# Where two chunks' layer-3 projections are asked for: in the first attention block of layer 1, or ahead of its group norm

## The chip, the cores and the metric

One core of a Trainium2 chip runs the whole program. Its engines work side by side, each through a queue of its own in order: PE (TensorE, matrix products), DVE (VectorE), ACT (ScalarE), POOL (GpSimd), and SP (SyncE), which here issues DMAs. The metric is the device time of one execution in microseconds (us); lower is better. Everything is float32.

## What is computed

Four layers on four images of 64 x 64 pixels with 128 channels. Layer 0 is neighbourhood attention with a 7 x 7 window, layer 1 a group norm and full attention over all 4096 pixels, layer 2 a gated mixing with a layer norm, layer 3 a scan in four directions (behind a projection and a 3 x 3 depthwise convolution). Cut to what this change touches:

```python
x = L0(x)                                  # neighbourhood attention
# layer 1
h = group_norm(x, gn_scale, gn_bias)       # 32 groups, statistics over a whole image
q, k, v = h @ wq + bq, h @ wk + bk, h @ wv + bv
o = softmax(q k^T / sqrt(128)) v
x = x + o @ wo + bo
x = L2(x)
# layer 3, its front
xz = x @ Win                               # 128 -> 512
xb, z = split(xz)                          # 256 channels each
xb = silu(depthwise_conv_3x3(xb) + conv_b)
...                                        # four scans, gate by silu(z), layer norm, Wout
```

The group norm needs the mean and the variance over a whole image, so layer 1 of an image can't begin before the last block of its layer 0.

## The kernel before

The images go one after the other through layers 0 to 2, and the scan of layer 3 comes behind all of them. What layer 3 needs before its scan (projection, convolution, gate, in the program "the front") is spread over the attention of layer 1: while image `b` is in layer 1, the front works on the second half of the image ahead (`b - 1`, chunks 4 to 7) and on the first half of `b`. A chunk is 8 image rows, 512 pixels. For image 0 there is no image ahead, so the first four places of the front are empty there.

Layer 0 of an image (`layer_0`) takes 32 blocks of 128 pixels. For each it makes scores (PE, L458), adds the bias and takes the maximum (DVE, L462), the exponential (ACT, L476), divides (POOL, L484), transposes the weights (PE, L493; copied out by ACT or DVE at L495), multiplies with the values (PE, L504; ACT L509) and projects (PE, L514; DVE L515). Every fourth block four finished tiles are transposed into `hT` (PE L413, ACT L414) and their statistics taken (DVE L417). Many of these instructions are pinned to the order in which the program asks for them.

Layer 1 (`layer_1`) then does the group norm, a chain of small steps that wait for each other: L556 (DVE, statistics of the image) -> L559 (PE, over groups) -> L561, L563, L565 (DVE) -> L567 (PE) -> L569 (DVE) -> L570 (ACT, square root, with a load of its table ahead of it) -> L572, L573 (DVE) -> L582 (DVE, eight times, the normalised `hT`) -> L584, L587, L591 (PE, queries, keys and values of eight chunks). After that come 32 blocks of attention: `score` (PE L613, copied out by ACT L616, maximum on DVE L619, L624), `turn_maxima` (PE L628, DVE L630 and L632), `soften` (PE L636, DVE L639, ACT L640) and `value` (PE L646). The maximum of a block is turned during the block behind it, and its values are multiplied in the block behind that one, so block 0 has scores alone and block 1 scores and the turn.

Behind block `i` the function `between(i)` asks for work of layer 2 and calls `first_part(i)`, which is the front's `turn(i)`. In a turn, `project` makes a chunk's projection: two matmuls (L788, 128x512, two records in the trace each), two copies into the tile `xh` (ACT L789) and the rows at the seam to the neighbouring chunk (POOL L792 to L795). `convolve` asks for the convolution of a chunk in four parts: ACT begins the sum (L831) and makes four of the nine products (L846, L850), POOL adds those (L858, L861), and DVE does the other four (L867, `add_taps`, called "taps" below). `gate` (L817) is the other half of the projection. `add_parts` asks for the POOL additions of the turn before.

The order within an engine's queue is not that of the program text: a scheduler places an instruction where it expects its inputs, by the order of the asking, except for those that are pinned. What is asked for early can so be placed early, with all that hangs on it.

The tiles of the front lie in the places of layer 0's bias tables (`xh` in the place "be", the sums `acc` in "bm0" and "bm2"), so nothing can be written into `xh` before layer 0's last L462 has read its bias.

Before the change, `first_part(-1)` loads the two chunks (L782) ahead of `layer_1`, and `turn(0)`, behind block 0, projects them:

```python
        first_part = front(b)
        first_part(-1)
        layer_1(b, xt, *handed.pop(b), between)
```

Of the kernel before, what the change touches and what calls it, by code (L numbers as in the profile page):

```python
# [75 lines left out]
def region(n, dy, dx):  # L76

    return max(0, -dy - RC * n), min(RC, H - dy - RC * n), max(0, -dx), min(W, W - dx)
# [60 lines left out]
def layers_0_to_2(  # L139
# [619 lines left out]
    def by_image_rows(t):  # L759
        return t.rearrange("p (i j) -> p i j", j=W)  # L760

    def front(b):
# [6 lines left out]
        def at_end(i, n):  # L769
            return i == B - 1 and n >= 4  # L770

        def by_product(i, n):


            return n == 3 or at_end(i, n)

        def load(i, n):
            if at_end(i, n):
                x_of[i, n] = fresh.pop(n)
                return  # L780
            x = x_of[i, n] = tmp.tile([P, CH], F32, name="xc", tag="g1")
            nc.sync.dma_start(x, x3_d[i][:, bass.ts(n, CH)])  # L782

        def project(i, n):
            me = n & 1
            for f in range(2):
                pi = ps_s([P, CH], "pi")
                nc.tensor.matmul(pi, lhsT=win[:, P * f:P * f + P], rhs=x_of[i, n], start=True, stop=True)  # L788
                nc.scalar.copy(xh[:, me, f, 1:RC + 1, :], by_image_rows(pi))  # L789
            row = nc.vector if at_end(i, n) and n > 5 else nc.gpsimd  # L790
            if n == 4 and i < b:
                nc.gpsimd.tensor_copy(xh[:, me, :, 0, :], kept_row)  # L792
            elif n > 0:
                row.tensor_copy(xh[:, me, :, 0, :], xh[:, 1 - me, :, RC, :])
                row.tensor_copy(xh[:, 1 - me, :, RC + 1, :], xh[:, me, :, 1, :])  # L795

        def project_row(i, n):

            me = n & 1
            x = tmp.tile([P, W], F32, name="xr", tag="oT")  # L800
            nc.sync.dma_start(x, x3_d[i][:, CH * n:CH * n + W])
            pi = ps_t([P, 2, W], "pr3")
            for f in range(2):
                nc.tensor.matmul(pi[:, f, :], lhsT=win[:, P * f:P * f + P], rhs=x, start=True, stop=True)
            nc.scalar.copy(xh[:, 1 - me, :, RC + 1, :], pi)
            nc.gpsimd.tensor_copy(kept_row, xh[:, 1 - me, :, RC, :])
# [6 lines left out]
        def gate(i, n):  # L813
            x = x_of.pop((i, n))
            for f in range(2):
                pz = ps_s([P, CH], "pz")
                nc.tensor.matmul(pz, lhsT=win[:, DI + P * f:DI + P * f + P], rhs=x, start=True, stop=True)  # L817
                zf = tmp.tile([P, CH], F32, name="zf", tag="c512", bufs=9)

                silu(i, n, zf, pz)  # L820
                nc.sync.dma_start(zf_d[i][f][:, bass.ts(n, CH)], zf)
# [11 lines left out]
        def taps(i, n):  # L833


            v = (1, 0) if n < NCH - 1 else (-1, 0)
            gp, ve = [v, (-1, 1), (1, -1), (1, 1)], [(-v[0], 0), (0, -1), (0, 1), (-1, -1)]
            return (gp[:2], ve + gp[2:]) if i == B - 1 and n in (5, 7) else (gp, ve)
# [14 lines left out]
        def add_parts():  # L853
            for i, n, f, k, p in parts_of:
                of = taps(i, n)[0]
                r0, r1, c0, c1 = region(n, *of[k])
                a = by_image_rows(sums[n, f])[:, r0:r1, c0:c1]
                nc.gpsimd.tensor_tensor(a, a, p, ALU.add)  # L858
                if k == len(of) - 1:
                    acc = accs[n & 1][:, f, :]  # L860
                    nc.gpsimd.tensor_tensor(acc, acc, sums.pop((n, f)), ALU.add)  # L861
            parts_of.clear()
# [33 lines left out]
        def activate(i, n, apart=False):  # L896
            if apart:
                u_of[i, n] = [tmp.tile([P, CH], F32, name="u1", tag="c512", bufs=9) for _ in range(2)]
                for f in range(2):
                    if i == B - 1 and (n, f) in ((6, 0), (6, 1), (7, 0)):  # L900
                        nc.scalar.activation(u_of[i, n][f], sums.pop((n, f)), AF.Silu, bias=cl("conv_b", f))
                    else:
                        silu(i, n, u_of[i, n][f], accs[n & 1][:, f, :])
            else:
                u_of[i, n] = [u0[:, f, :] for f in range(2)]
                silu(i, n, u0, accs[n & 1])
# [6 lines left out]
        def copy_du(i, n):  # L913

            m = (L - CH * (n + 2)) // SC
            for f in range(2):
                for b2 in range(B):
                    if b2 != i - 1:
                        nc.sync.dma_start(y_d[(i ^ b2) >> 1][b2][f][m], y_d[(i ^ (i - 1)) >> 1][i - 1][f][m])
# [37 lines left out]
        def times_b(i, n, bb, engine):  # L957
            for f, u in enumerate(u_of.pop((i, n))):
                engine.tensor_tensor(u, u, bb, ALU.mult)
                nc.sync.dma_start(ub_d[i][f][:, bass.ts(n, CH)], u)  # L960
# [37 lines left out]
        takes = [[(b - 1, 4), (b - 1, 5)], [(b - 1, 6)], [(b - 1, 7)]] if b > 0 else [[], [], []]  # L998
# [4 lines left out]
        def convolve(i, n, fs, half):  # L1003
            for f in fs:
                if half == 0:
                    begin(n, f)
                multiply(i, n, f, range(len(taps(i, n)[0]))[2 * half:2 * half + 2])
            for f in fs if half else []:
                add_taps(i, n, f)
# [49 lines left out]
        def turn(i):  # L1059

            j, r = divmod(i, 4)
            add_parts()
            if i == -1:
                for c in takes[0]:
                    load(*c)
                return
            now = whole[j] if j < 8 else None
            if j < 8:
                if r == 0:
                    for c in takes[j]:  # L1070
                        project(*c)
                    if j == 7 and b < B - 1:
                        project_row(b, 4)
                if now and j < 7:
                    convolve(*now, (r // 2,), r & 1)
                elif now and r < 2:
                    convolve(*now, range(2), r)
                if r == 3:
                    for c in takes[j]:
                        gate(*c)  # L1080
                    for c in takes[j + 1] if j < 7 else []:
                        load(*c)

            for k, at in ((0, 16), (2, 28), (4, 32)):
                if i == at and whole[k] and whole[k][0] & 1:
                    copy_du(*whole[k])
            if b > 0 and i == 8 and (b - 1) & 1:
                copy_du(b - 1, 2)

            for c, at in zip(whole, u_at):  # L1090
                if c and i == at:
                    activate(*c, at >= 32)
                if c and i == at + 1:
                    lower(*c)
                if c and i == at + 2 and not by_product(*c):
                    times_b(*c, x_of.pop((*c, "b")), nc.gpsimd)
            if b > 0 and i in (22, 24):
                turn_c(b - 1, (i - 22) // 2)
            if b == 0 and i == 3:
                output_weights()  # L1100
            if b == B - 1 and i == 6:
                diagonals()
            if b == B - 1:
                end(i)
# [7 lines left out]
    for b in range(B):  # L1112
        xt = ahead.pop(0)
        for _ in coming:
            pass
        parts = layer_2(b, xt)

        def between(i):

            n, part = divmod(i - 6, 4)  # L1120
            if i == 6 and b + 1 < B:
                ahead.append(load_x(b + 1))
            if i >= 6 and n < NCH:
                parts[part](n)
            first_part(i)
            if b + 1 < B and i == NT + 1:
                edge_of[b + 1] = edge_bias(0)
            if b + 1 < B and i == NT + 3:
                bias_m[:] = bias_tiles()
                for t, d in zip(bias_m, bias_d):  # L1130
                    nc.sync.dma_start(t, d)

        first_part = front(b)
        first_part(-1)
        layer_1(b, xt, *handed.pop(b), between)
        if b + 1 < B:
            coming = layer_0(b + 1, ahead[0], edge_of[b + 1])
        for i in range(NT + 2, NT + 6 if b + 1 < B else NT + 11):
            between(i)
            if b + 1 < B:  # L1140
                next(coming)
                next(coming)
# [380 lines left out]
```

## Time and profile before

| | |
|---|---|
| median of 3 runs | 3720.32 us (3720.11 to 3721.49) |
| the profiled execution's own time | 3719.04 us |
| span of its instructions | 3717.3 us |
| busy in the span: PE, DVE, ACT, POOL | 90%, 75%, 73%, 38% |
| granted PE clock over the span | 0.916 |
| start of the group norm (L556), images 0 to 3 | 209.26, 933.95, 1684.75, 2435.65 us |
| first L582, images 0 to 3 | 212.31, 937.11, 1687.92, 2438.81 us |
| L788 | 592 ns a record, x112 (chunks read from DRAM) |

The page tells busy time by engine, then the span in 40 slices, queues, the chain that ended last, the costliest groups of instructions by line, and DMA issues. A line of the timeline reads: start in us, length in us, engine, line, operation, output<-input, shapes, how many, and in brackets the idle time ahead of it and what ended it. Lengths of neighbours overlap: the next of a row begins some 0.1 us before the end of the one ahead, so what a queue pays for one instruction is read from start to start. A table by stretches gives for each A:B (us from the span's start) its length, then for each engine the busy time and the number of instructions that began in it, the granted PE clock and the DMA share.

### The profile page before, as it was taken

Reading aid. Unit: us, or ns where it says so; the run is one execution under the profiler, and the core shown is the slowest. Engines: PE = TensorE matmul, PEld = TensorE weight load, DVE = VectorE, ACT = ScalarE, POOL = GpSimd, SP = SyncE. Lnnn points to the kernel's source line nnn. Section 1 sums busy time; section 2 is a strip of 40 time slices with the busy share of each in tenths; the row PEclk is TensorE's granted clock in tenths of the full one; section 3 lists DMA queues with packets and bytes.
Section 4 is the critical chain, followed back from the end, with each engine's and each line's share of the span. In section 5 each row is a group of like instructions: output and inputs, shape, how many; then the busy total and the mean of one; then the engine's idle time right before and its main releaser. Section 6 shows DMA issues by size and latency. Waiting matters only on the chain. (4 is left out here: it accounts for less than half of the span.)

```text
span 3717.3 us, 70142 instructions
## 1 busy us (share of the span) xinstructions
PE 3357.8 (90%) x26774; PEld 2775.6 (75%) x26774; DVE 2794.8 (75%) x5227; ACT 2700.4 (73%) x4387; POOL 1422.9 (38%) x1592
## 2 busy tenths in 40 slices
PE   6999999999999999998999999989999997666647
PEld 3779999967799999677999997779899962222236
DVE  3667878866677788666777886667787777999968
ACT  3865677778677777786677776867767778999934
POOL 5600012245121222451122223522221337999956
PEclk7999999999999999999999999999999995555579
DMA  4200000131011012410121212100100259999998
GB/s 130 63 3 26 13 18 30 45 99 40 10 49 35 32 41 82 127 45 1 47 77 30 72 51 98 47 1 24 43 31 33 70 168 240 219 232 210 210 275 281
DMA packets 188308, 310.95 MB, mean 84 GB/s; under 512 B 22303, under 2 KB 110908, under 8 KB 183068
## 3 DMA queue, kind: packets, MB, share of 16 engines
q1 hardware_dynamic: 144068, 220.79, 17.6%
q0 software_dynamic: 24384, 76.95, 11.6%
q10 hardware_dynamic: 19520, 8.73, 0.8%
q8 instruction: 211, 3.46, 0.4%
q14 instruction: 125, 1.02, 0.1%
HBM read 167.69 MB, written 155.56 MB: 87 GB/s over the span
## 5 line engine op out<-in xcount | busy, mean ns | idle before, releaser
L613 PE MATMUL sc<-qT,kT 128*128 128x128 f32 x8192 | 1083.8, 276 | 15.6 <-DVE mx L619 15.6
L646 PE MATMUL po<-v,st 128*128 128x129 f32 x8192 | 1082.7, 275 | 2.0 <-ACT st L640 2.0
L613 PEld LDWEIGHTS sc<-qT,kT 128*128 128x128 f32 x8192 | 1000.8, 193 | 38.4 <-issue 26.6
L646 PEld LDWEIGHTS po<-v,st 128*128 128x128 f32 x8192 | 1000.1, 192 | 4.7 <-ACT st L640 2.2
L616 ACT COPY st<-sc 128x512 f32<-128x512 f32 x1024 | 574.8, 584 | 426.0 <-PE sc L613 425.4
L619 DVE TENSOR_TENSOR mx<-mx,sc 128x512 f32<-128x512 f32 x768 | 524.7, 683 | 201.8 <-ACT st L616 178.2
L639 DVE TENSOR_TENSOR st<-st,pb 128x2048 f32<-128x2048 f32 x256 | 574.6, 2281 | 5.2 <-PE pb L636 4.1
L640 ACT ACTIVATE st<-st 128x2048 f32<-128x2048 f32 x256 | 483.1, 1908 | 64.5 <-DVE st L639 63.8
L1233 PE MATMUL pdt<-dbl,dt 8*128 8x512 f32 x512 | 307.3, 1079 | 140.9 <-ACT de L1240 140.6
L1244 POOL TENSOR_TENSOR inp<-de,ub 128x1024 f32<-128x1024 f32 x128 | 411.1, 4431 | 9.4 <-DMA ub_d<-u 5.3
L1233 PEld LDWEIGHTS pdt<-dbl,dt 8*128 8x128 f32 x512 | 114.1, 312 | 331.2 <-ACT de L1240 269.0
L484 POOL TENSOR_SCALAR pr<-pr,sm 128x308 f32<-128x308 f32 (+3 forms) x512 | 244.7, 497 | 221.0 <-DVE sm L482 187.6
L712 POOL TENSOR_TENSOR x<-x,row 128x512 f32<-128x512 f32 x32 | 40.8, 1275 | 695.1 <-PE pt L275 695.1
L858 POOL TENSOR_TENSOR gsum<-gsum,tp 128x504 f32<-128x504 f32 (+1 forms) x177 | 240.9, 1364 | 170.1 <-ACT tp L850 82.2
L476 ACT ACTIVATE pr<-pr,mx 128x308 f32<-128x308 f32 (+3 forms) x512 | 262.6, 517 | 0.0
L1271 DVE TENSOR_TENSOR_SCAN h<-h,end,inp 128x1024 f32<-128x1024 f32 x96 | 221.2, 2346 | 17.5 <-ACT h L1257 7.5
L462 DVE CUSTOM_DVE_ANT_0 pr<-sc,bias_m 128x266 f32<-128x266 f32 (+1 forms) x384 | 152.0, 452 | 107.4 <-PE sc L458 100.9
L493 PE MATMUL pt<-ident,pr 128*88 128x128 f32 (+5 forms) x1472 | 204.4, 276 | 7.8 <-ACT prT L495 7.8
L1286 POOL DMA_DIRECT2D y<-yo x112 | 203.0, 2755 | 9.4 <-DVE yo L1285 7.3
L867 DVE SCALAR_TENSOR_TENSOR acc<-xh,cc,acc 128x512 f32<-128x512 f32 (+3 forms) x250 | 200.0, 821 | 4.6 <-ACT acc L831 3.6
L493 PEld LDWEIGHTS pt<-ident,pr 128*88 128x88 f32 (+5 forms) x1472 | 164.2, 138 | 45.1 <-ACT prT L495 31.6
L495 ACT COPY prT<-pt 110x512 f32<-110x512 f32 (+3 forms) x240 | 139.1, 580 | 65.0 <-PE pt L493 64.0
(234 smaller groups left out, 5178.8 us busy)
## 6 DMA issues: line engine op xcount, KB each, us to landing
y<-yo POOLq DMA_DIRECT2D x112, 512.0 KB, 10.9
y<-y SPq DMA_DIRECT2D x48, 512.0 KB
zf_d<-zf SPq DMA_DIRECT2D x64, 256.0 KB
ub_d<-u SPq DMA_DIRECT2D x64, 256.0 KB
ub<-ub_d SPq DMA_DIRECT2D x16, 1024.0 KB
yl<-y SPq DMA_DIRECT2D x64, 256.0 KB
zc<-zf_d SPq DMA_DIRECT2D x64, 256.0 KB
x<-in_x SPq DMA_DIRECT2D x128, 64.0 KB
```

The source lines that it names most:

```text
L476: pin(nc.scalar.activation(k.pr[:, h], k.pr[:, h], AF.Exp, bias=k.mx[:, h:h + 1], accum_out=k.sm[:, h:h + 1]))
L484: nc.gpsimd.tensor_scalar(k.pr[:, h], k.pr[:, h], k.sm[:, h:h + 1], 1.0, ALU.mult, ALU.mult)
L493: pin(nc.tensor.transpose(pt[0:n, h, :], k.pr[:, h, at:at + n], ident))
L613: nc.tensor.matmul(ps[:, r, :], lhsT=kT[:, bass.ts(G * g + r, P)], rhs=qT[:, bass.ts(i, P)], start=True, stop=True)
L616: nc.scalar.copy(k.st[:, G * g:G * g + G, :], ps)
L619: nc.vector.tensor_tensor(k.mx, k.st[:, 0:G, :] if g == 1 else k.mx, ps, ALU.max)
L639: nc.vector.tensor_tensor(part, part, pb.unsqueeze(1).to_broadcast([P, 16, P]), ALU.add)
L640: nc.scalar.activation(part, part, AF.Exp)
L646: nc.tensor.matmul(k.po, lhsT=k.st[:, j, :], rhs=v[:, j, :], start=(j == 0), stop=(j == NT - 1))
L858: nc.gpsimd.tensor_tensor(a, a, p, ALU.add)
L1233: nc.tensor.matmul(pdt[j][:, g, :], lhsT=dt[o:o + RANK, P * f:P * f + P], rhs=at(dbl[o:o + RANK, :], k & 2, g0, g0 + CH), start=True, stop ...
L1244: nc.gpsimd.tensor_tensor(by_rows(inp), by_rows(de), at(ub_s[f], b ^ (k & 1), SC * n, SC * n + SC), ALU.mult)
```

## The change

```diff
         def turn(i):
             j, r = divmod(i, 4)
-            add_parts()
+            if i >= 0:
+                add_parts()
+            if i == -2:
+                for c in takes[0]:
+                    load(*c)
+                return
             if i == -1:
                 for c in takes[0]:
-                    load(*c)
+                    project(*c)
                 return
             now = whole[j] if j < 8 else None
             if j < 8:
                 if r == 0:
-                    for c in takes[j]:
+                    for c in takes[j] if j > 0 else []:
                         project(*c)
...
         for _ in coming:
             pass
+
+        first_part = front(b)
+        first_part(-2)
+        first_part(-1)
         parts = layer_2(b, xt)
...
-        first_part = front(b)
-        first_part(-1)
         layer_1(b, xt, *handed.pop(b), between)
```

`takes[0]` holds chunks 4 and 5 of the image ahead (empty for image 0). They are loaded at the new turn -2 and projected at turn -1, both behind the last block of layer 0 and ahead of the group norm; turn 0 projects nothing any more. The convolution is asked for where it was. In the built program this moves, for images 1 to 3:

- PE: the four L788 stand among the last products of layer 0 (L493, L504) and no longer behind the scores of block 0.
- ACT: the four L789, and with them four L831, two L846 and seven L850 of the two chunks' convolution, stand among layer 0's last copies and ahead of the table load of L570. In the kernel before they stood among the copies of blocks 0 to 2.
- DVE: all 16 taps (L867) of the two chunks. Of the first chunk's eight, seven stand among layer 0's last steps, the eighth between the last L417 and L556. Of the second chunk's, one stands between L565 and L569, four between L569 and L572, one each ahead of L573 and of L582, one behind the L582.
- POOL: one row copy (L794) ahead of the division (L484) for the last block, the other (L795) behind it, and the first addition (L858) ahead of the memset L579.
- SP: the same instructions in the same order.

From L582 on through blocks 0 to 2, the instructions of PE, ACT and DVE for images 1 to 3 now stand in the same order as those of image 0, apart from one tap behind the L582 and a few short ones at the end of block 2.

## The prediction

> **What bounds the kernel now.** I began with the page's busy shares, which say that PE is the fullest engine and so that work taken off a stretch where PE sets the pace should pay. Then I compared stretches: from the first L582 to the end of block 2 of layer 1, for image 0 (no chunks of an image ahead) and for images 1 to 3 (two chunks). Each stretch ends just ahead of the 193rd record of L613; 192 records are three blocks of scores. The columns are length, PE busy, weight loads busy, clock, DMA.
>
> ```profile
> PE 3357.8 (90%) x26774; PEld 2775.6 (75%) x26774; DVE 2794.8 (75%) x5227; ACT 2700.4 (73%) x4387; POOL 1422.9 (38%) x1592
> ```
>
> ```profile
> 212.31:268.20 55.89, 23.47 (x192) 22.47 (x193) 0.96 0.00 1
> 937.11:1001.45 64.34, 24.74 (x192) 23.66 (x193) 0.92 0.00 1
> 1687.92:1752.36 64.44, 24.68 (x192) 23.64 (x193) 0.92 0.00 1
> 2438.81:2503.24 64.43, 24.66 (x192) 23.59 (x193) 0.92 0.00 1
> ```
>
> The same scores take 8.5 us more in images 1 to 3. The timeline of PE for image 3 shows where: 3.6 us of L788, and waits for DVE, which has taps between the steps of the turned maximum. (Of the wait of 3.26 us, image 0 has 2.6 us too.)
>
> ```profile
> 2470.54 3.60 PE L788 MATMUL pi<-xc,win 128*128 128x512 f32 x8
> 2480.01 0.49 PE L636 MATMUL pb<-dm,ones 128*128 128x128 f32 x2 [1.52 <-DVE dm L632]
> 2485.76 1.36 PE L613 MATMUL sc<-qT,kT 128*128 128x128 f32 x8 [3.26 <-DVE mx L619]
> ```
>
> Behind block 2 the timeline shows PE without a gap in block 3, so taps there cost nothing now. Last I read the place the work goes to, the end of layer 0 and the group norm, on ACT and DVE. Every gap in brackets is short and belongs to one chain: copy, product, copy, last L414, L417, statistics, root, L582.
>
> ```profile
> 2428.73 0.58 ACT L495 COPY prT<-pt 66x512 f32<-66x512 f32 x1 [0.72 <-PE pt L493]
> 2432.69 0.27 ACT L509 COPY oT<-po 128x128 f32<-128x128 f32 x1 [1.14 <-PE po L504]
> 2434.30 0.59 ACT L414 COPY hT<-pt 128x512 f32<-128x512 f32 x1 [1.35 <-PE pt L413]
> 2434.91 1.28 ACT L570 ACT_TABLE_LOAD   x1
> 2435.65 0.37 DVE L556 BATCH_NORM_AGGREGATE mv<-st 128x2 f32<-128x48 f32 x1
> 2437.99 0.16 DVE L569 TENSOR_SCALAR sd<-pvar 128x1 f32<-128x1 f32 x1 [0.68 <-PE pvar L567]
> 2438.41 0.16 DVE L572 RECIPROCAL ga<-sd 128x1 f32<-128x1 f32 x1 [0.27 <-ACT sd L570]
> ```
>
> **What goes away: blocks 0 to 2.** The moved work is all that distinguishes these blocks from image 0's, and image 0's order of instructions is what they now have. So the gain is the difference of the stretches: (64.34 + 64.44 + 64.43) / 3 - 55.89 = 8.5 us an image, if PE's clock behaves as in image 0.
>
> **The clock.** Behind the group norm's pause PE runs at half speed:
>
> ```profile
> 212.31:216.66 4.35, 3.75 (x5) 1.69 (x6) 3.74 (x8) 0.69 (x1) 0.00 (x0) 0.50 0.00 0
> 2438.81:2445.56 6.75, 6.15 (x14) 3.57 (x15) 4.36 (x9) 1.38 (x2) 0.00 (x0) 0.50 0.01 2
> ```
>
> Image 0 has 3.75 us of PE work at half clock, image 3 has 6.15 us; half of each is lost, 1.9 and 3.1 us. That is 1.2 us of the 8.5. The records change the clock at a grid: its spells at half speed last 3.41, 6.83 and 10.24 us. In both images the clock came back behind the first whole step of 3.41 us in which PE worked. Where the restart falls on the grid after the change I can't say to a microsecond, so the half-speed work is 3.4 to 6.8 us, middle 5.1: 2.55 us lost, 0.65 more than in image 0. The gain is 8.5 - 0.65 = 7.85 us, between 8.65 (3.4 us) and 7.0 (6.8 us).
>
> The Trainium skill ("TensorE: Matmul & The Clock Gate", section "HAM oscillation — how this bites in real kernels") speaks against the change here: no pauses of PE over some 3.4 us, or the clock is halved again. PE's pause is longer than that already in the rows (from 2434.3 to 2439.4, clock 0.61 then 0.50), so a longer one changes only how the restart falls on the grid. Were the rule's cost a new one, half of a busy step of 3.4 us would be lost again in each image, 1.7 us, and the sum below would be 3 x (-1.6 + 1.7) = +0.3, that is 3720.6; by the rows it is paid already, and the sum is -4.8.
>
> **What is added: the end of layer 0 and the group norm.** Prices from start to start, from the rows of blocks 0 and 1 of image 3:
>
> ```profile
> 2473.14 3.75 DVE L867 SCALAR_TENSOR_TENSOR acc<-xh,cc,acc 128x512 f32<-128x512 f32 x5 [0.30 <-ACT acc L831]
> 2474.97 0.83 ACT L831 ACTIVATE acc<-xh,col,cc 128x512 f32<-128x512 f32 x1
> 2475.69 0.72 ACT L846 ACTIVATE gsum<-xh,cc 128x512 f32<-128x512 f32 x1
> 2476.30 1.56 ACT L616 COPY st<-sc 128x512 f32<-128x512 f32 x3
> 2477.72 0.75 ACT L850 ACTIVATE tp<-xh,cc 128x504 f32<-128x504 f32 x1
> 2478.34 0.61 ACT L616 COPY st<-sc 128x512 f32<-128x512 f32 x1
> 2478.61 2.60 POOL L858 TENSOR_TENSOR gsum<-gsum,tp 128x504 f32<-128x504 f32 x2 [0.61 <-ACT tp L850]
> ```
>
> L831 0.72, L846 and L850 0.62, a copy 0.48 (1.42 for three); a tap 0.73 where it follows a tap on the same sum (five end 3.67 us on), 0.65 otherwise; an addition 1.3.
>
> *ACT, up to the last L414.* Ahead of it stand 4 copies, 2 L831, 2 L846 and 4 L850: 4 x 0.48 + 2 x 0.72 + 6 x 0.62 = 7.1 us. From 2424.09 (first inserted copy) to 2434.30 ACT idles six times between its copies, 4.3 us by the brackets (0.30, 0.72, 0.29, 0.50, 1.14, 1.35), and 0.7 more since a successor that is ready starts 0.12 earlier than the end of the one ahead. So 5.0 are covered and L414 comes 2.1 us later. I followed PE and DVE alongside: the four L788 (0.86 each) go through PE's gaps, seven taps fit into DVE's waits for products that are late anyway, and ACT stays the one that sets the pace. The two copies ahead of block 31's exponentials put its division on POOL back 0.9 us; its transposes on PE then come at about 2431.7, ahead of ACT's need at 2432.5.
>
> *DVE, from the last L417 to L582.* One tap ahead of L556: 0.65, less the 0.12 that L556 waited, 0.55. One between L565 and L569 takes the place of a wait of 0.68: 0.05. Four between L569 and L572: 0.1 + 2 x 0.73 + 2 x 0.65 = 2.9 where 0.42 were, 2.45. One each ahead of L573 and L582, 0.55 each. Sum 4.15 us, since DVE takes its queue in order and the chain stands behind the taps. The last one, behind the eight L582, is hidden by PE's products: L592 waits over 2 us for the first.
>
> *ACT and POOL ahead of the root.* Behind L414 stand 3 L850, 2 L831 and the table load: 0.48 + 3 x 0.62 + 2 x 0.72 + 1.28 = 5.1 us, so the root can come at 2436.4 + 5.1 = 2441.5. DVE needs it at L572, which its taps put at some 2443.4: 1.9 us to spare. The third of these L850 reuses the place of a product that POOL adds third. The first L846 ends near 2433.7, three additions and the memset take 4.1: 2437.8, against 2438.8 when ACT arrives. With 1.9 us behind it, POOL may be 2.9 late before it costs anything; then everything behind is late one for one.
>
> Loss: 2.1 + 4.15 = 6.25 us an image. Bounds: 4.15 if ACT's part is covered wholly; 16 taps x 0.73 = 11.7 if no tap finds a free DVE. I take 6.25, since the order of the queues fixes its terms and the waits were read one by one. SP's queue doesn't change; the loads of L782 were issued 20 us ahead of the first L788 and stay there.
>
> **Sum.** 6.25 - 7.85 = -1.6 us an image, three images: -4.8. The profiled execution's span of 3717.3 becomes 3712.5, its own time 3719.04 (1.7 outside the span) 3714.2; the median of the runs lies 1.3 above that execution: 3715.5.
>
> **Rivals.**
> 1. *The end of layer 0 swallows ACT's share.* Then only DVE's 4.15 are lost: 3 x (4.15 - 7.85) = -11.1, 3709.2. For it: PE and ACT both have gaps there. Against: 7.1 us don't go into 5.0.
> 2. *The taps stand in the chain of the group norm with no cover.* DVE's 16 taps at 0.73 are 11.7 us an image; 3 x (11.7 - 7.85) = +11.6, 3731.9, slower. For it: seven of the second chunk's eight taps are between steps that wait for each other. Against: DVE idles 1.5 to 2 us at a time in the end of layer 0. It decides from a loss of 7.85 us on, when some 2 more of the first chunk's seven covered taps find no gap.
> 3. *The stall in blocks 0 to 2 stays*, so that only L788 leaves PE (3.44 us by its starts): 3 x (6.25 - 3.44) = +8.4, 3728.7. Against it: image 0 runs the same order of instructions without it. That the projections aren't moved at all is excluded by the built order.
>
> **Chances.** My sum, with loss and gain a microsecond off either way, gives -10 to +2, 3710 to 3722: 0.64. Rival 1: 0.17. Rival 2: 0.13. Rival 3: 0.06. Some 0.2% (7.4 us) is about what a measurement of this kernel can tell from no change. Faster by more than that (below 3712.9): rival 1 and the lower edge of mine, 0.26. Slower (above 3727.8): most of rivals 2 and 3, 0.14. Within: 0.60. For 8 in 10 the range takes in half of the way to rivals 1 and 2: 3708 to 3726.
>
> **What would show it.** In the profile after, for images 1 to 3: the stretch from the first L582 to the 193rd score takes 56 to 58 us; from layer 0's last L476 to the last L414 it takes some 9 us (7.9 before), L556 to L582 takes 6.75 us (3.16 before), the root waits for nothing after its table load and L572 follows a tap at once. The prediction is wrong if L556 to L582 exceeds 8 us, if ACT stands ahead of the table load waiting for POOL, or if blocks 0 to 2 still hold a wait of L636 for L632.

## The result, and the profile after

The changed kernel takes 3734.52 us (median of 6 runs, 3730.71 to 3736.54), the kernel before beside it 3720.22 (6 runs, 3714.58 to 3721.49): 1.0040 of the time, 95% interval 1.0027 to 1.0053. It is slower, and outside the range of the forecast. The profiled execution has a span of 3731.9 us, 14.6 more than before.

The page's first part for the kernel after, busy us (share of the span) of each engine:

```profile
PE 3349.5 (90%) x26774; PEld 2770.1 (74%) x26774; DVE 2806.9 (75%) x5227; ACT 2700.4 (72%) x4387; POOL 1426.7 (38%) x1592
```

The counts are those of before. PE is 8.3 us less busy, as less of its work falls at half clock (in each of images 1 to 3, between the end of layer 0 and block 2, some 10.7 us of it before and 5.6 after); PE lost time waiting, not working. DVE is busy for 12.1 us more and POOL for 3.8 us more with the same instructions: some of them take longer. That is where to look.

First the gain. Windows of L613 in the kernel after, images 1 to 3, from the first L582 to the 193rd score record (length, PE busy, weight loads busy, clock, DMA):

```profile
948.50:1004.80 56.30, 23.46 (x192) 22.54 (x193) 0.95 0.00 1
1702.90:1759.17 56.27, 23.47 (x193) 22.54 (x193) 0.96 0.00 1
2457.27:2513.68 56.41, 23.47 (x192) 22.54 (x193) 0.96 0.00 1
```

56.3 us where 64.4 were: 8.1 gained in each image, and the blocks now run like those of image 0 (55.9). So the loss lies ahead of the first L582. DVE's timeline in the kernel after, around the group norm of image 3 (start, length, engine, line, operation, operands, count; in brackets the idle time ahead and what ended it):

```profile
2436.87 2.31 DVE L867 SCALAR_TENSOR_TENSOR acc<-xh,cc,acc 128x512 f32<-128x512 f32 x3 [0.27 <-ACT acc L831]
...
2441.21 0.73 DVE L867 SCALAR_TENSOR_TENSOR acc<-xh,cc,acc 128x512 f32<-128x512 f32 x1
...
2442.40 2.85 DVE L867 SCALAR_TENSOR_TENSOR acc<-xh,cc,acc 128x504 f32<-128x504 f32 x2
2445.18 0.68 DVE L417 BATCH_NORM_STATS2 st<-hT 128x6 f32<-128x512 f32 x1
2445.78 1.13 DVE L867 SCALAR_TENSOR_TENSOR acc<-xh,cc,acc 128x504 f32<-128x504 f32 x1
2446.84 0.36 DVE L556 BATCH_NORM_AGGREGATE mv<-st 128x2 f32<-128x48 f32 x1
2447.88 0.16 DVE L561 COPY gm<-pm 128x1 f32<-128x1 f32 x1 [0.68 <-PE pm L559]
2448.07 1.20 DVE L563 TENSOR_TENSOR dv<-mv,gm 128x1 f32<-128x1 f32 x1
2449.30 1.29 DVE L565 SCALAR_TENSOR_TENSOR vv<-dv,mv 128x1 f32<-128x1 f32 x1
2450.51 0.74 DVE L867 SCALAR_TENSOR_TENSOR acc<-xh,cc,acc 128x512 f32<-128x512 f32 x1
2451.27 0.16 DVE L569 TENSOR_SCALAR sd<-pvar 128x1 f32<-128x1 f32 x1
2451.34 4.56 DVE L867 SCALAR_TENSOR_TENSOR acc<-xh,cc,acc 128x504 f32<-128x504 f32 x4
2455.83 0.15 DVE L572 RECIPROCAL ga<-sd 128x1 f32<-128x1 f32 x1
```

POOL's timeline of the same kernel over the same stretch:

```profile
2440.86 2.20 POOL L858 TENSOR_TENSOR gsum<-gsum,tp 128x504 f32<-128x504 f32 x1 [1.53 <-ACT gsum L846]
2443.00 0.15 POOL L579 MEMSET v<- 128x32 f32 x1
2443.14 3.23 POOL L858 TENSOR_TENSOR gsum<-gsum,tp 128x504 f32<-128x504 f32 x2
2446.45 1.59 POOL L861 TENSOR_TENSOR acc<-acc,gsum 128x512 f32<-128x512 f32 x1
2448.00 4.36 POOL L858 TENSOR_TENSOR gsum<-gsum,tp 128x504 f32<-128x504 f32 x3
```

DVE's timeline of the kernel before, the same two steps:

```profile
2436.89 0.16 DVE L563 TENSOR_TENSOR dv<-mv,gm 128x1 f32<-128x1 f32 x1
2437.09 0.22 DVE L565 SCALAR_TENSOR_TENSOR vv<-dv,mv 128x1 f32<-128x1 f32 x1
```

Read them together. Until POOL's additions begin at 2440.86 three taps take 2.31 us, 0.77 each. From then on two take 2.85, one 1.13, four 4.56. L563, one number per partition, takes 1.20 us instead of 0.16, L565 1.29 instead of 0.22. L556 (one input) and L561 and L569 (input from a matmul's result) stand among them at their usual lengths. Two taps there take 0.73 and 0.74 (at 2441.21 and 2450.51), and there it is the additions that are long: 2.20 us for one, then three in 4.36, where an addition takes 1.25 to 1.3 when DVE does nothing of this kind.

The lengths of the stretches, the same in images 1 to 3 within 0.1 us:

| us an image | before | after | change | predicted |
|---|---|---|---|---|
| layer 0's last L462 to the last L414 | 13.25 | 15.60 | +2.35 | +2.1 |
| last L414 to L556 | 1.35 | 3.55 | +2.20 | +0.55 |
| L556 to the first L582 | 3.16 | 10.43 | +7.27 | +3.6 |
| blocks 0 to 2 | 64.4 | 56.3 | -8.1 | -7.85 |
| sum | | | +3.7 | -1.6 |

Three images make +11.1 of the 14.6. The rest is net of small differences elsewhere and of +4.6 in what comes behind the last L646, the scan above all (689.6 us before, 694.2 after). That code is the same in all kernels of this study and took 689.1 to 693.7 us in the nine others, so I attribute nothing there.

### The profile page after: what moved, and what is told of

Its sections match the earlier page's. It is cut to its first block, busy times and chain, and to the rows that moved or that the text cites. A ratio compares the mean times of both kernels' runs of the same rounds, so it can differ in the third digit from the quotient of the medians.

```text
span 3731.9 us, 70155 instructions
## 1 busy us (share of the span) xinstructions
PE 3349.5 (90%) x26774; PEld 2770.1 (74%) x26774; DVE 2806.9 (75%) x5227; ACT 2700.4 (72%) x4387; POOL 1426.7 (38%) x1592
## 3 DMA queue, kind: packets, MB, share of 16 engines
q14 instruction: 125, 1.02, 0.1%
## 5 line engine op out<-in xcount | busy, mean ns | idle before, releaser
L613 PE MATMUL sc<-qT,kT 128*128 128x128 f32 x8192 | 1079.3, 276 | 13.6 <-DVE mx L619 13.6
L646 PE MATMUL po<-v,st 128*128 128x129 f32 x8192 | 1080.6, 275 | 2.0 <-ACT st L640 2.0
L613 PEld LDWEIGHTS sc<-qT,kT 128*128 128x128 f32 x8192 | 997.0, 192 | 34.9 <-issue 23.9
L646 PEld LDWEIGHTS po<-v,st 128*128 128x128 f32 x8192 | 997.8, 192 | 4.7 <-ACT st L640 2.2
L619 DVE TENSOR_TENSOR mx<-mx,sc 128x512 f32<-128x512 f32 x768 | 524.4, 683 | 212.4 <-ACT st L616 187.6
L639 DVE TENSOR_TENSOR st<-st,pb 128x2048 f32<-128x2048 f32 x256 | 574.5, 2280 | 6.7 <-PE pb L636 5.7
L640 ACT ACTIVATE st<-st 128x2048 f32<-128x2048 f32 x256 | 483.1, 1908 | 64.4 <-DVE st L639 63.7
L484 POOL TENSOR_SCALAR pr<-pr,sm 128x308 f32<-128x308 f32 (+3 forms) x512 | 243.8, 496 | 219.3 <-DVE sm L482 190.6
L858 POOL TENSOR_TENSOR gsum<-gsum,tp 128x504 f32<-128x504 f32 (+1 forms) x177 | 244.1, 1383 | 145.1 <-ACT gsum L846 83.2
L462 DVE CUSTOM_DVE_ANT_0 pr<-sc,bias_m 128x266 f32<-128x266 f32 (+1 forms) x384 | 152.0, 452 | 112.9 <-PE sc L458 104.2
L795 POOL COPY xh<-xh 128x128 f32<-128x128 f32 x23 | 10.1, 439 | 584.4 <-ACT xh L789 580.0
L867 DVE SCALAR_TENSOR_TENSOR acc<-xh,cc,acc 128x512 f32<-128x512 f32 (+3 forms) x250 | 207.7, 853 | 4.5 <-ACT acc L831 3.5
L493 PE MATMUL pt<-ident,pr 128*88 128x128 f32 (+5 forms) x1472 | 203.3, 275 | 6.2 <-ACT prT L495 6.2
L1293 POOL DMA_DIRECT2D y<-yo x112 | 200.7, 2715 | 11.1 <-DVE yo L1292 5.5
L493 PEld LDWEIGHTS pt<-ident,pr 128*88 128x88 f32 (+5 forms) x1472 | 164.0, 138 | 45.1 <-ACT prT L495 30.7
```

Of the source, the lines that this page charges most:

```text
L493: pin(nc.tensor.transpose(pt[0:n, h, :], k.pr[:, h, at:at + n], ident))
L613: nc.tensor.matmul(ps[:, r, :], lhsT=kT[:, bass.ts(G * g + r, P)], rhs=qT[:, bass.ts(i, P)], start=True, stop=True)
L619: nc.vector.tensor_tensor(k.mx, k.st[:, 0:G, :] if g == 1 else k.mx, ps, ALU.max)
L639: nc.vector.tensor_tensor(part, part, pb.unsqueeze(1).to_broadcast([P, 16, P]), ALU.add)
L640: nc.scalar.activation(part, part, AF.Exp)
L646: nc.tensor.matmul(k.po, lhsT=k.st[:, j, :], rhs=v[:, j, :], start=(j == 0), stop=(j == NT - 1))
```

## The experiments

Theory A: POOL's additions and DVE's instructions with two inputs from SBUF hold each other out, so the one waits while the other reads. Theory B: the taps themselves stand in the chain and cost what they cost, whatever POOL does (the forecast's second rival). All kernels start from the kernel after, but for `e4_before_held`. Ratios are to the kernel before, run beside them (3720.38 to 3722.23).

**No additions.** For the two chunks POOL adds nothing; the taps stay.

```diff
-                nc.gpsimd.tensor_tensor(a, a, p, ALU.add)
+                if i == b or n > 5:
+                    nc.gpsimd.tensor_tensor(a, a, p, ALU.add)
                 if k == len(of) - 1:
                     acc = accs[n & 1][:, f, :]
-                    nc.gpsimd.tensor_tensor(acc, acc, sums.pop((n, f)), ALU.add)
+                    s = sums.pop((n, f))
+                    if i == b or n > 5:
+                        nc.gpsimd.tensor_tensor(acc, acc, s, ALU.add)
```

> The changed kernel without POOL's additions (L858, L861) for the two chunks of the image ahead; the sums lack these four products. Theory A (a tap and an addition that both read SBUF hold each other back, so the taps cost 1.1 to 1.4 us and L563, L565 over 1 us): taps return to 0.65 to 0.73 us, L563 and L565 to 0.2, L556 to L582 to 6.8 us (10.4 in the changed kernel), last L414 to L556 to 1.9 (3.55); some 5.3 us an image, 3718 us. Theory B (the taps are slow because the chain's steps between them wait for PE and ACT, the additions have no part in it): L556 to L582 stays above 9.5 us and the time above 3730.

3713.26 us, ratio 0.9981 [0.9971, 0.9991], 5 us less than theory A's 3718. DVE's timeline, image 3 (the taps' line is L870 here):

```profile
2430.84 1.51 DVE L870 SCALAR_TENSOR_TENSOR acc<-xh,cc,acc 128x504 f32<-128x504 f32 x2
...
2434.80 0.16 DVE L563 TENSOR_TENSOR dv<-mv,gm 128x1 f32<-128x1 f32 x1
2434.99 0.22 DVE L565 SCALAR_TENSOR_TENSOR vv<-dv,mv 128x1 f32<-128x1 f32 x1
2435.97 2.71 DVE L870 SCALAR_TENSOR_TENSOR acc<-xh,cc,acc 128x504 f32<-128x504 f32 x4
```

Four taps take 2.71 us instead of 4.56, and L563 and L565 have their old lengths. The last L414 to L556 takes 1.86 us, L556 to L582 6.47; the stretch ahead stays at 15.60. The loss is now 6.17 us an image, against the forecast's 6.25. B would have left it at 11.8, and the time above 3730.

**No taps.** For the two chunks DVE makes no taps; POOL's additions stay.

```diff
-            for dy, dx in taps(i, n)[1]:
+            for dy, dx in taps(i, n)[1] if i == b or n > 5 else []:
```

> The changed kernel without DVE's 16 taps for the two chunks of the image ahead; the sums lack these products. Additions stay early. Theory A: L563 and L565, which read two SBUF tiles, still wait for additions, some 1 us each, while L561, L569, L572 do not; L556 to L582 is 5 to 5.5 us. Theory B: nothing is left in the chain's way, L556 to L582 is 3.2 us. Both: last L414 still some 2.3 us later than before, since ACT's work stays; about 3708 us by A, 3702 by B.

3713.87 us (one run), more than either theory said. L556 to L582 takes 4.39 us: below A's number, above B's. Blocks 0 to 2 take 57.5 us instead of 56.3; the eight L582 at their start last 2.0 us longer. DVE's timeline, image 3:

```profile
2433.11 0.57 DVE L563 TENSOR_TENSOR dv<-mv,gm 128x1 f32<-128x1 f32 x1
2433.72 1.17 DVE L565 SCALAR_TENSOR_TENSOR vv<-dv,mv 128x1 f32<-128x1 f32 x1
2435.57 0.16 DVE L569 TENSOR_SCALAR sd<-pvar 128x1 f32<-128x1 f32 x1 [0.68 <-PE pvar L567]
...
2436.39 5.69 DVE L582 TENSOR_SCALAR hT<-hT,gm,ga 128x512 f32<-128x512 f32 x8
```

POOL's timeline of this kernel:

```profile
2432.40 1.27 POOL L861 TENSOR_TENSOR acc<-acc,gsum 128x512 f32<-128x512 f32 x1
2433.63 1.25 POOL L858 TENSOR_TENSOR gsum<-gsum,tp 128x504 f32<-128x504 f32 x1
```

With no tap near, L563 ends at 2433.68, when the addition that began at 2432.40 ends, and L565 runs from there to 2434.89, when the next one ends. These are whole waits, not a slower rate. The eight L582 take 5.69 us instead of 3.74 beside the additions that follow, so they are held too, though each reads but one tile.

**POOL busy, but reading nothing.** Each addition for the two chunks becomes one memset of `gsum`, then three, so that POOL is at work as long as with the additions.

```diff
-                nc.gpsimd.tensor_tensor(a, a, p, ALU.add)
+                if i == b or n > 5:
+                    nc.gpsimd.tensor_tensor(a, a, p, ALU.add)
+                else:
+                    nc.gpsimd.memset(a, 0.0)
...
```

> The changed kernel with POOL's additions for the two chunks replaced by memsets of the same tiles, which write SBUF and read nothing; the sums are not those of the reference. Theory A (what holds DVE is a shared way of reading SBUF): taps at 0.65 to 0.73 us, L563 and L565 at 0.2, L556 to L582 6.5 us as without additions; 3713 us. Theory C (any instruction of POOL that touches SBUF holds DVE): taps at 1 us and more while the memsets run, L556 to L582 8 us or more, 3725 us or more.

> The changed kernel with each of POOL's additions for the two chunks replaced by three memsets of the same tile, so that POOL is busy as long as with the additions and beside the whole group norm, but reads nothing; the sums are not those of the reference. Theory A: taps at 0.65 to 0.73 us, L563 0.16, L565 0.22, L556 to L582 6.5 us, about 3712 us. Theory C (POOL's activity as such holds DVE): taps over 1 us, L563 and L565 near 0.5 (one memset), L556 to L582 8 us or more, 3720 us or more.

One memset: 3711.87 us, ratio 0.9970 [0.9959, 0.9981], taps of 0.73 us beside memsets of 0.52. But POOL was done before L563, so that this run said nothing of the chain; hence three. Three: 3714.53 us, 0.9981 [0.9971, 0.9990]. POOL's and then DVE's timeline with three, image 3 (taps: L876):

```profile
2433.27 6.73 POOL L862 MEMSET gsum<- 128x504 f32 x14
```

```profile
2438.24 0.16 DVE L563 TENSOR_TENSOR dv<-mv,gm 128x1 f32<-128x1 f32 x1
2438.43 0.22 DVE L565 SCALAR_TENSOR_TENSOR vv<-dv,mv 128x1 f32<-128x1 f32 x1
2439.41 2.70 DVE L876 SCALAR_TENSOR_TENSOR acc<-xh,cc,acc 128x504 f32<-128x504 f32 x4
```

POOL works without a gap from 2433.27 to 2440.00 and writes `gsum` as the additions do, and L563, L565 and the taps keep their lengths; L556 to L582 takes 6.60 us. So it isn't POOL's being busy, nor its writing, that holds DVE. What an addition does and a memset doesn't is to read. In the same trace a row copy of POOL (L794, 0.29 us), which does read, runs from 2442.72, and L573, which has two inputs from SBUF and begins at 2442.74, takes 0.28 us instead of 0.16.

**The convolution held back.** The chunks' products and taps are pinned behind the blocks that ask for them, so that only L788 and its copies move (`e1_conv_held`); the same pins on the kernel before (`e4_before_held`).

```diff
+        def hold(n, ins):
+            return tc.keep_in_program_order(ins) if moved and n in (4, 5) else ins
...
-            nc.scalar.activation(acc, x, AF.Identity, bias=cl("conv_b", f), scale=c)
+            hold(n, nc.scalar.activation(acc, x, AF.Identity, bias=cl("conv_b", f), scale=c))
...
-                nc.vector.scalar_tensor_tensor(acc, x, c, acc, ALU.mult, ALU.add)
+                hold(n, nc.vector.scalar_tensor_tensor(acc, x, c, acc, ALU.mult, ALU.add))
...
+                moved[:] = [1] if j < 2 else []
```

> The changed kernel with the convolution of the two chunks (L831, L846, L850 on ACT and the taps on DVE, the additions with them) held at the place where it is asked for, behind the blocks of layer 1; the projections alone go ahead. Theory A and B: L556 to L582 back to 3.2 us, the loss is that of four copies on ACT, 1 to 1.5 us an image; the four L788 (3.44 us) leave block 0. If the stall in blocks 1 and 2 stays whole, gain 3.4: 3714 us; if it goes too, 8.1: 3700 us.

> The kernel before with the convolution of the same chunks held where it is asked for; the projections stay behind block 0. If the stall of blocks 1 and 2 came from taps placed ahead of the turned maximum by the scheduler, this alone takes up to 4 us an image (3708 us); if the taps stall PE wherever they stand in blocks 1 and 2, nothing (3720 us, within 4).

The first takes 3725.48 us, 1.0004 [0.9995, 1.0013]: my expectation missed. The group norm is as short as expected (L556 to L582 2.95 us), and up to block 5 an image gains 2.8 us (3.2 in image 3). But then images 1 and 2 lose 5.1 us each and image 3 2.6 (from the 4th to the 8th L650 73.4, 73.4 and 71.0 us, 68.3 before), in the blocks at whose turns the second chunk's products and taps are pinned. The second takes 3725.25, 1.0011 [1.0002, 1.0021], with the same losses. Its stretches from the first L582 to the 193rd score record take 64.0, 64.3 and 61.1 us, against 64.4 before and 56.3 after. Pinning the convolution alone doesn't take the stall away.

**A split.** The first chunk's sum is begun (L831) ahead of the group norm and its taps stay free to go there; its other products, and with them POOL's additions, are pinned at turns 0 to 3; the second chunk is begun and tapped at turns 2 and 3.

```diff
...
                     project(*c)
+                for f in range(2) if b > 0 else []:
+                    begin(4, f)
                 return
...
+                moved[:] = [1] if j < 1 else []
+                if j == 0 and now and r > 1:
+                    begin(5, r - 2)
+                    add_taps(b - 1, 5, r - 2)
...
```

> The changed kernel, with the projections ahead of the group norm as there, but of the convolution only the beginning (two L831) and the taps of the first chunk go ahead; its products on ACT, and so POOL's additions, are held behind block 0 of layer 1, and the second chunk's beginning and taps are asked for at turns 2 and 3 and held there. The result is the reference's. By theory A: no addition runs beside a tap or the group norm; last L414 some 1 us later, one tap ahead of L556, L556 to L582 3.2 us: loss 1.5 to 2 us an image. Gain 8 less what ACT's products cost blocks 1 and 2, 0 to 2 us: 3700 to 3707 us. If the taps in the end of layer 0 cost by themselves (theory B), no better than 3712.

3708.73 us (5 runs, 3707.79 to 3715.06), 0.9968 [0.9956, 0.9981]: the upper end of what I expected was 3707, but it is faster than both kernels. DVE's timeline, image 3 (taps: L874):

```profile
2429.24 0.72 DVE L874 SCALAR_TENSOR_TENSOR acc<-xh,cc,acc 128x504 f32<-128x504 f32 x1
...
2430.91 0.16 DVE L563 TENSOR_TENSOR dv<-mv,gm 128x1 f32<-128x1 f32 x1
...
2432.83 3.74 DVE L582 TENSOR_SCALAR hT<-hT,gm,ga 128x512 f32<-128x512 f32 x8
```

One tap is left in the chain, L556 to L582 takes 2.95 us here, and no row of it is held. From layer 0's last L462 to the end of block 9, images 1 to 3 gain 6.2 us together; the spans differ by 10.3, and the rest lies in stretches where the split moves nothing. By the score records of image 3 the third and fourth block take 16.8 and 19.7 us, 2.0 and 1.6 more than in the kernel after.

Two kernels looked for those 3.6 us and for more ahead of the group norm: the second chunk's taps left free, and on top of that its projection held until layer 0's last transposes are copied.

```diff
...
-                    project(*c)
+                    if c[1] == 5:
+                        with tc.issue_after(last_of[0]), tc.issue_after(last_of[1]):
+                            project(*c)
+                    else:
+                        project(*c)
...
```

> The split version, with the second chunk's taps no longer held: they are asked for at turns 5 and 7 as in the changed kernel, and only the beginning they build on (L831) is held, at turns 2 and 3. The result is the reference's. If the 3.6 us that blocks 2 and 3 still lose in the split version (16.8 and 19.7 us against 14.8 and 18.1 in the changed kernel) come from four taps standing together ahead of the turned maximum, they shrink to 1 us: some 2.5 us an image less, 3701 us. If ACT's products in these blocks cost them, no change, 3709.

> As the version before it, with the second chunk's projection queued behind layer 0's last transposes on PE and its two copies behind the last L414 on ACT, in the pause of the group norm. Two copies and a wait less ahead of the last L414 (0.9 us earlier), no tap ahead of the statistics (0.6 us), the root 0 to 0.5 us later behind two copies: 0.5 to 1.5 us an image less than the version before it, and PE's clock may come back earlier since its pause is shorter.

3710.50 us, 0.9975 [0.9966, 0.9985], and 3711.03, 0.9975 [0.9964, 0.9985]. Left free, the taps were placed where they had been pinned, and the two blocks took 16.8 and 19.65 us, as long. The later projection shortens the last L414 to L556 to 1.64 us and L556 to L582 to 2.75, but the last L414 itself comes 0.1 us later, not 0.9 earlier, and the time shows no gain.

What lengthens the third block is in the trace, and it is neither ACT's products nor DVE's taps: POOL's additions, pinned there, stand beside L624, which takes the maximum of two halves of one tile in SBUF. POOL's, DVE's and PE's timelines of the split, image 3 (POOL's additions: L865):

```profile
2477.12 2.65 POOL L865 TENSOR_TENSOR gsum<-gsum,tp 128x504 f32<-128x504 f32 x2 [10.22 <-ACT tp L857]
2477.42 2.50 DVE L624 TENSOR_TENSOR mx<-mx 128x256 f32<-128x256 f32 x2
2479.97 0.33 PE L628 MATMUL pt<-ident,mx 128*128 128x128 f32 x1 [1.94 <-DVE mx L624]
```

The same two L624 take 0.43 and 0.29 us in the kernel after, and PE's wait of 1.94 us is the block's 2.0. In the fourth block one L624 beside an addition takes 1.34 us instead of 0.28, four taps stand with it, and PE waits 1.02 us for L632; how the 1.6 us divide there stays open.

## Why the prediction was wrong

*The step that failed* is the loss' second term, "DVE, from the last L417 to L582", 4.15 us. Its places were right and its prices were not: 0.65 to 0.73 us a tap, and L563 and L565 at no more than before. They came from rows that no addition lengthens (of the five taps quoted, the last meets the start of one, and then it is the addition that takes longer, 1.51 us), while the same prediction moves the additions to the same stretch and prices those, too, at a row of their own (1.3). Measured, the two stretches grow by 9.5 us. Of these, 1.3 lie ahead of the last L417, where the forecast had nothing: the last two of the seven taps that were to fit into DVE's waits take 2.85 us together, and L417 starts 1.89 us behind the start of the last L414 instead of 0.62. Without the additions they grow by 0.51 + 3.31 = 3.8, so the step's 4.15 is about right for a DVE left alone, and 5.6 us an image is the price of POOL reading beside it. By rows, L556 to L582: L563 1.20 for 0.16, L565 1.29 for 0.22, four taps 4.56 for 2.71, 3.96 more in all, which is the difference between 10.43 and the 6.47 of the run without additions.

The trace of before had the row: the next tap behind the five I quoted. DVE's and POOL's timelines of the kernel before, block 1 of image 3:

```profile
2477.01 1.54 DVE L867 SCALAR_TENSOR_TENSOR acc<-xh,cc,acc 128x504 f32<-128x504 f32 x1
...
2479.07 0.89 DVE L632 TENSOR_SCALAR dm<-ident,nm 128x128 f32<-128x128 f32 x1
```

```profile
2476.49 1.51 POOL L858 TENSOR_TENSOR gsum<-gsum,tp 128x504 f32<-128x504 f32 x1 [0.89 <-ACT gsum L846]
```

A tap of 1.54 us beside an addition of 1.51. And L632, 0.89 us beside the next addition (at 2478.61) and 0.28 in the kernel after: the 0.81 and 0.61 us by which the two are too long make 1.4 of the 1.52 us for which PE's L636 waits there. The stall that the change removes, which the forecast put down to the taps as such, was in part this hold already. Over the whole trace of before, 193 taps with no two-input instruction of POOL's (TENSOR_TENSOR) beside them have a mean of 0.73 us, none above 0.75, and 57 that overlap one 1.13; after, 178 have 0.73 and 72 have 1.17. Had I priced the seven taps of this step that have no wait to go into at 1.13 instead of some 0.69, the loss would have been 6.25 + 7 x 0.44 = 9.3 us, and three times 9.3 - 7.85 makes some +4.4: a slower kernel. L563 and L565 would still have been missing.

The Trainium skill states the rule ("SBUF — State Buffer", section "Who interferes with whom"): "A DVE instruction with two SBUF inputs contends with a GpSimd instruction that reads SBUF", not with one that only writes it, and the lock is exclusive. The runs agree with each part: L563 1.20 us beside additions and 0.16 beside memsets, L569 0.16 beside either, and without taps L563 and L565 end when the addition beside them ends. The page excepts DVE's two-port modes from what it says of instructions with one input; whether L582, held in the kernel without taps, is such a case no run here shows.

*The gain* was right: 8.1 us an image against 7.85. The third rival, that the stall stays, falls with the 56.3 us.

*The clock* was right. Windows of the kernel after, all engines (length, then busy of PE, weight loads, DVE, ACT, POOL, then clock):

```profile
2443.29:2457.27 13.98, 1.18 (x4) 1.00 (x4) 13.18 (x19) 5.51 (x9) 11.11 (x8) 0.57 0.00 0
2457.27:2462.26 4.99, 4.40 (x8) 2.35 (x9) 4.38 (x10) 1.27 (x2) 0.00 (x0) 0.50 0.01 3
```

The stretch in which PE has next to no work grew from some 5 to 14 us, and the restart still has only 4.40 us of work at half clock, inside the 3.4 to 6.8 named. For PE's clock the longer pause cost nothing more.

*ACT up to the last L414*: +2.35 against +2.1, the same without additions, and the first rival, that the gaps swallow it, is excluded. But the size came out in part by luck. In `e1_conv_held` ACT has only the four copies more there, none of the L831, L846 and L850 (5.2 of the 7.1 us), and 1.70 of the 2.35 stay (14.95 us). PE's timeline of that kernel shows no wait from the first L788 (2428.44) to 2439.7, and ACT waits for PE:

```profile
2436.81 0.59 ACT L789 COPY xh<-pi 128x512 f32<-128x512 f32 x1 [0.71 <-PE pi L788]
```

So the four L788 don't simply go through PE's gaps, as the forecast said; with them alone PE sets the pace, and the convolution on ACT and DVE adds 0.65. That ACT alone sets it in the kernel after isn't shown.

*ACT ahead of the root* had time to spare, as predicted, though ACT waited for POOL (0.28 and 0.24 us), which I named as a sign against it. The root did not follow its table load at once, as I had said; it waits for L569, which is late itself. ACT's timeline after:

```profile
2446.41 0.72 ACT L850 ACTIVATE tp<-xh,cc 128x504 f32<-128x504 f32 x1 [0.24 <-POOL gsum L858]
2447.84 1.28 ACT L570 ACT_TABLE_LOAD   x1
2451.46 0.20 ACT L570 ACTIVATE sd<-sd 128x1 f32<-128x1 f32 x1 [2.33 <-DVE sd L569]
```

These waits go into the 2.33 that the root then waits for DVE.

*The second rival* (a loss of 11.7 us, 3731.9) comes close to the measured 11.8 by another cause: without the additions the seven taps do find free time in layer 0 (L417 starts 0.60 us behind the start of the last L414, as before), with them five do, and 16 at 0.73 us was the sum of another story. Its size alone would have passed for a proof; the run without additions tells the two apart.

## What to carry to other kernels

A duration from a trace holds for its neighbours: before taking a price for a DVE instruction with two inputs from SBUF, look at what POOL does beside that row and what it will do at the new place. Moving two streams that read SBUF, one on each of these engines, into one stretch costs both, and small two-input steps of a serial chain pay the most for their size. Beside the chain of this group norm (L556 to L582 3.16 us) the taps alone cost 3.3 us and the additions alone 1.2, both together 7.3: if something has to stand beside such a chain, let it be one of the two.

## What the runs showed of the hardware

The size of it: a 128x1 L563 lasts until the 128x504 addition beside it ends, 1.20 us for 0.16. And that an instruction with one tile and numbers per partition as inputs is also held: eight L582 5.69 us for 3.74, and over the whole trace of before an L632 0.96 us on average where it overlaps a TENSOR_TENSOR of POOL's, 0.28 elsewhere. L624, with two inputs from SBUF, takes 1.4 us for 0.42 at 128x256. L619 and L639, with one input from SBUF and one from a matmul's result, keep their 0.68 and 2.28 us either way.
